# A four-layer graph network on one core: six of its 32 units keep their rows in SBUF between layers, and the output is laid out by node, then batch

## The chip, the core and the metric

The kernel runs on one core of one Trainium2 chip. A core has five engines that run their own instruction lists in order: TensorE (PE, matrix products, with its weight loads shown as PEld), VectorE (DVE), ScalarE (ACT), GpSimd (POOL) and SyncE (SP), which here only starts transfers. Transfers run on the core's 16 DMA engines, whichever list started them. SBUF is the on-chip memory of 128 partitions, PSUM the smaller one that PE writes to, DRAM the memory outside. The metric is the device time of one execution in microseconds (us); lower is better.

## The reference, cut to what matters

The input is x of shape (8, 2048, 128): 8 batches, 2048 nodes, 128 features. adj is a symmetric 0/1 matrix of 2048 x 2048 with ones on the diagonal and some 17 neighbours a node. Four layers follow each other: two of attention with a feed-forward part (layers 0 and 2, "MHA" here) and two of graph attention (layers 1 and 3, "GAT").

```python
# MHA, layers 0 and 2 (8 heads of 16)
Q, K, V = (h @ Wq), (h @ Wk), (h @ Wv)              # split into heads
scores = einsum('bnhd,bmhd->bhnm', Q, K) / sqrt(16)
attn = softmax(where(adj == 0, -inf, scores))
x = layer_norm(h + (attn @ V) @ Wo + bo, ln1_g, ln1_b)
x = layer_norm(x + relu(x @ W1 + b1) @ W2 + b2, ln2_g, ln2_b)

# GAT, layers 1 and 3
h = x @ W
e = leaky_relu((h @ a_src)[:, :, None] + (h @ a_dst)[:, None, :], 0.2)
att = softmax(where(adj == 0, -inf, e))
x = layer_norm(att @ h + x, ln_gamma, ln_beta)
```

## The kernel before, in words

The kernel (class Sparse; a class Dense stands behind a branch for matrices with too many neighbours, and is not run here) uses that adj is sparse. The nodes are cut into 32 units of 64 nodes (UNIT). Each unit has a list of its neighbours, built at the start from adj (block_list, unit_list), padded to 9 tiles of 128 slots (TILES), which are worked off in five steps of two, two, two, two and one tile.

Each layer first needs a table in DRAM with a row for each node: for MHA the keys and values of all 8 batches (8192 bytes), for GAT the projected features with two extra columns (4160 bytes). For each tile, POOL starts an indirect transfer (gather, line 1473) that fetches the 128 rows of the tile's slots from the table into a buffer kv of SBUF. There are six such buffers; one holds two tiles of an MHA layer or four of a GAT layer.

In MHA (attention) a step is: PE spreads the queries to the slots (qe, line 1546), DVE multiplies them with the keys (line 1558) and adds up over each head (line 1565), ACT takes the exponential (line 1575), POOL or DVE multiplies it with the values (line 1584), and PE adds the slots up for each node (line 1614). In GAT (graph) DVE makes the score e (line 1778, then 1785), ACT takes its exponential (1790), DVE folds it into the one-hot matrix of targets, giving w (line 1800), and PE adds up with w as its weights (line 1815). After its last step a unit is finished (after_attention, after_graph): products, normalisation, and at the end of layers 0 to 2 the unit's new rows x, transposed (xnew, from scaled, lines 1453 and 1455), and their projection for the next layer's table (project), which SP stores (line 1396). A layer's gathers need the whole table, so layers don't overlap, but for the loads of x and of the one-hot matrices.

The unit's rows x are needed again in the next layer, as queries' input and for the residual sum. So keep (line 1229) stores xnew, 256 KB, into a DRAM array xd, and in the next layer fetch (line 1241) loads it into one of four buffers x. Both transfers are on SP's list. In the last layer the normalised rows are stored into the output array of shape (8, 2048, 128) by two transfers of 128 KB a unit (line 1876), one for each half of the batches; a partition holds one node of one half, 4 batches x 128 features, and its four pieces of 512 bytes go to four places.

The order of all instructions is made beforehand by a planner (class Plan): each operation has a cost in us for each engine that may run it, a key (its due place), and the buffers it takes; the planner runs through them in simulated time and writes each engine's list in the order that results. A pool of buffers that is empty delays the operations that need one. The transfers have a cost in the plan too, so a transfer that is left out can move other operations. Within the lists the hardware runs in order, and semaphores do the waiting.

Names that the change touches: SBUF_BUFS (buffers of each pool; "w" has 3, "x1" 2 and "at" 1, the last two used in after_attention alone, 2 KB a partition each), keep, fetch, scaled, the fold in graph, the store in after_graph, falling (a constant row of 2048 numbers of 16 bits, read by block_list alone), zeros (a constant that nothing reads), and kernel, which makes the output array and hands it back.

Of the kernel before, what the change touches and what calls it, by code (L numbers as in the profile page):

```python
# [9 lines left out]
F32 = mybir.dt.float32  # L10
F32R = mybir.dt.float32r
BF16 = mybir.dt.bfloat16
# [8 lines left out]
P = 128  # L21
# [4 lines left out]
CH = 512  # L26
# [6 lines left out]
GROUP = 32  # L33
UNIT = 2 * GROUP
TG = 5
TILES = 2 * TG - 1
GS = TG * P
FIRST = 4
DEG = 40
KV = 4 * 1024 + 128  # L40
HOT = GS + 2 * TG * GROUP
WIDE = DEG + 5
STRIDE = 1000
LEAD = 60

SBUF_BUFS = {
    "kv": 6, "hot": 3, "hot8": 2, "x": 4, "q_sb": 2, "rows": 3, "at": 1, "r": 2, "x1": 2, "hidden": 1, "normed": 2,
    "xnew": 2, "trows": 2, "s": 2, "var": 2, "rstd": 2, "rc": 2, "te": 2, "e": 4, "w": 3,
    "cand": 2, "aux": 3, "unit_aux": 2, "some": 2, "rank_e": 2, "pick": 1,
}  # L50
BY_KEY = ("kv", "hot", "x", "q_sb", "acc")
# [14 lines left out]
class Dense:  # L66
# [460 lines left out]
    def batch(self, b):  # L527
        x = self.two.tile([P, self.NB, P], F32, name="x")
        self.nc.sync.dma_start(out=x, in_=self.x_in[b].rearrange("(t p) d -> p t d", p=P))
        for n, kind in enumerate(LAYERS):  # L530
            if kind is MHA:
                units = 2 * self.NB * (self.N // QC)
                gen = self.attention(x, n)
            else:
                units = self.NB * self.NC
                gen = self.graph(x, n)
            for u in gen:
                yield u / units
        self.nc.sync.dma_start(out=self.out[b].rearrange("(t p) d -> p t d", p=P), in_=x)

    def run(self):

# [199 lines left out]
class Sparse:  # L742
# [15 lines left out]
    def __init__(self, ctx, tc, x, xt, adj, w, out):  # L758
        self.tc, self.nc, self.w, self.xt_in, self.out = tc, tc.nc, w, xt, out
        self.B, self.N, _ = x.shape  # L760
        self.NB = self.N // P
        self.NU = self.N // UNIT
        self.HB = self.B // 2

        def pool(name, **kw):
            return ctx.enter_context(tc.tile_pool(name=name, **kw))

        self.nc.scalar.preload_act_table_set("natural_log_exp_and_others")
        self.const = pool("const", bufs=1)
# [24 lines left out]
        self.table = [Cell() for _ in LAYERS]  # L794

        self.xd = self.dram.tile([self.NU, P, CH], F32, name="xd")
        self.x_at = [Cell() for _ in range(self.NU)]
        self.hots = self.dram.tile([self.NU, P, HOT], F8, name="hots")
        self.hots_at = [Cell() for _ in range(self.NU)]
        self.ends_at = [None] * self.NU  # L800
        self.t = self.const.tile([P, self.NU, P // GROUP * self.HB], F32, name="t")
        self.t_at = [Cell() for _ in range(self.NU)]
        self.idx = self.const.tile([P, self.NU, TILES], I32, name="idx")
        self.idx_at = [Cell() for _ in range(self.NU)]

# [12 lines left out]
        self.rows_n = self.fixed("rows_n", float(self.N))  # L818
        self.huge = self.fixed("huge", 1e30)
        self.zeros = self.const.tile([GROUP, CH], BF16, name="zeros")  # L820
        self.nc.vector.memset(self.zeros, 0.0)

    def constants(self):
# [27 lines left out]
        for pattern, base, step, part in (  # L853
# [4 lines left out]
                part, pattern=pattern, base=base, channel_multiplier=step, allow_small_or_imprecise_dtypes=True  # L858
            )
        self.target = ramp("target", [P, GROUP], [[1, GROUP]], base=1)  # L860
        self.falling = const.tile([P, self.N], F16, name="falling")
        nc.gpsimd.iota(
            self.falling,
# [142 lines left out]
    def block_list(self, adj, i):  # L1006
# [21 lines left out]
                accum_out=self.seen[:, 0, i : i + 1],  # L1028
            ),
            key,  # L1030
            writes=[buf],
            port=True,
        )
# [190 lines left out]
            )  # L1224

    def keep(self, u, x, key):
        self.op(
            {"SP": 0.45},
            lambda e: e.dma_start(out=self.xd[u], in_=x.tile),
            key,  # L1230
            reads=[x],
            writes=[self.x_at[u]],
            dma=P * CH * 4,
        )

    def fetch(self, n, u, key):

        x = self.cell("x", [P, CH])
        self.op(
            {"SP": 0.45},  # L1240
            lambda e: e.dma_start(out=x.tile, in_=self.xd[u] if n else self.xt_in[u]),
            key,
            reads=[self.x_at[u] if n else self.gates[20]],
            writes=[x],
            dma=P * CH * 4,
        )
        hot = self.cell("hot", [P, HOT])
        if LAYERS[n] is MHA:
            hot8 = self.cell("hot8", [P, HOT], F8)
# [194 lines left out]
        else:  # L1444
            e.tensor_scalar(out, in_, by, None, ALU.mult)  # L1445

    def scaled(self, rows, gamma, beta, tag, key):
        x = self.cell(tag, [P, CH])
        ps = self.transposed(rows, key, x)

        def run(e):
# [9 lines left out]
            reads=[ps],  # L1461
# [163 lines left out]
    def after_attention(self, n, u, acc, sums, x, base):  # L1625
# [67 lines left out]
            )  # L1693
        add_to(r, ps, L["b2"], x1, key - 2)
        normed = self.norm(self.centred(r, key), key)
        x = self.scaled(normed, L["ln2_g"], L["ln2_b"], "xnew", key)
        self.keep(u, x, key)
        self.project(n + 1, u, x, key)

# [2 lines left out]
    def graph(self, n):  # L1702
# [3 lines left out]
        for u in range(self.NU):  # L1706
# [50 lines left out]
            for i, t in enumerate(steps):  # L1757
# [33 lines left out]
                    key - 4,  # L1791
                    writes=[e8],
                )
                w = cell("w", [P, 2, 2 * hb, GROUP])

                def fold(e, t=t, hot=hot, e8=e8, w=w, tiles=tiles):
                    oh = hot.tile[:, GS:HOT].rearrange("p (j t c) -> p j t c", j=2, t=TG)[:, :, t, :]
# [29 lines left out]
    def after_graph(self, n, u, outs, banks, acc, x, base):  # L1827
# [31 lines left out]
        )  # L1859
        normed = self.norm(r, key)  # L1860
        if n < len(LAYERS) - 1:
            x = self.scaled(normed, L["ln_gamma"], L["ln_beta"], "xnew", key)
            self.keep(u, x, key)
            self.project(n + 1, u, x, key)
        else:
# [8 lines left out]
            def store(e):  # L1874
                for part, nodes, hf in self.parts(u):
                    e.dma_start(
                        out=self.out[hf * hb : (hf + 1) * hb, nodes, :].rearrange("b p d -> p b d"),
                        in_=normed.tile[part],
                    )

# [102 lines left out]
```

## Time and profile before

| what | value |
|---|---|
| median of 3 runs (lowest, highest) | 3297.97 us (3291.01, 3309.48) |
| the profiled execution, its own time | 3274.86 us |
| its span, first to last instruction | 3273.1 us |
| PE, DVE, ACT, POOL busy, share of the span | 77%, 71%, 43%, 65% |
| moved by DMA | 1023.13 MB in 261243 packets |
| gathers (POOL's queue) | 864.44 MB, 70.8% of the 16 engines' time |
| SP's transfers | 154.56 MB, 13.8% |
| TensorE clock granted, mean | 0.875 of full speed |

The span has four stages. The lists and layer 0 go to about 1200 us, layer 1 to 1765, layer 2 to 2720, layer 3 to the end. Gathers of 8192-byte rows are those of layers 0 and 2, of 4160-byte rows those of 1 and 3. A line of "windows" gives for each engine the busy us in that stretch, then the granted clock, the mean busy share of the 16 DMA engines and the GB/s they moved. A line of "waits" reads: engine, line of the instruction that waited, what ended the wait, and then the total us, the number of waits and the longest one. In a line about a group of instructions, "x163" is how many there were, followed by shortest, median and longest duration in ns and the first and last start in us.

### The profile page before, as it was taken

The page shows a single profiled execution, that of the slowest core. Times are in us where ns is not written, and L with a number is a line of the kernel's source. Part 1 is how long each engine was busy: PE and PEld are TensorE (multiplying, and loading weights), DVE is VectorE, ACT ScalarE, POOL GpSimd, SP SyncE. Part 2 cuts the span into 40 slices and gives each one's busy share as a digit, 9 for nine tenths or more (in the row PEclk, how much of TensorE's full clock was granted, in tenths as well). Part 3 has the DMA queues.
Part 4 walks back from the last instruction along what each step waited for, and adds up shares of the span by engine and source line. Part 5 has one row for each costly group of instructions (what it writes and reads, how often), then busy time and mean ns, then how long its engine had stood idle before and what let it go on. Part 6 is the DMA issues. An engine that isn't in the chain of part 4 may idle for free. (4 is left out here: it accounts for less than half of the span.)

```text
span 3273.1 us, 63112 instructions
## 1 busy us (share of the span) xinstructions
PE 2517.2 (77%) x23560; PEld 1460.5 (45%) x23560; DVE 2308.8 (71%) x3740; ACT 1394.7 (43%) x4756; POOL 2131.7 (65%) x1454
## 2 busy tenths in 40 slices
PE   7768888888877767887876778888788785767675
PEld 5634444444333335565654333333333343555554
DVE  4779999898878753444445988988888883555555
ACT  4435554455444423444443344444444441333333
POOL 0268877787878725555553878877886854555662
PEclk8669999899999977889898899999999996778887
DMA  7858889788989849999997889989898866999994
GB/s 266 296 207 333 341 321 346 290 349 320 364 309 346 308 140 328 328 317 356 340 327 253 335 345 360 382 343 354 343 366 309 348 238 242 318 317 325 315 313 164
DMA packets 261243, 1023.13 MB, mean 313 GB/s; under 512 B 40192, under 2 KB 69632, under 8 KB 189024
## 3 DMA queue, kind: packets, MB, share of 16 engines
q0 software_dynamic: 166464, 864.44, 70.8%
q1 hardware_dynamic: 94464, 154.56, 13.8%
q8 instruction: 189, 3.10, 0.4%
q14 instruction: 126, 1.03, 0.1%
HBM read 978.59 MB, written 88.08 MB: 326 GB/s over the span
## 5 line engine op out<-in xcount | busy, mean ns | idle before, releaser
L1473 POOL DMA_INDIRECT kv<-table,idx x1152 | 1191.4, 1034 | 877.0 <-issue 359.9
L1584 POOL TENSOR_TENSOR kv<-kv 128x2048 f32<-128x2048 f32 (+1 forms) x259 | 927.2, 3593 | 85.3 <-ACT kv L1575 81.2
L1558 DVE TENSOR_TENSOR kv<-qe,kv 128x2048 f32<-128x2048 f32 (+1 forms) x320 | 662.6, 2071 | 156.5 <-DMA kv<-table,idx 104.6
L1565 DVE TENSOR_REDUCE s<-kv 128x128 f32<-128x2048 f32 (+1 forms) x320 | 659.9, 2062 | 8.5 <-ACT ps_e L1575 0.5
L1546 PE MATMUL qe<-q_sb,hot 32*128 32x512 f32 (+1 forms) x2304 | 401.8, 703 | 193.6 <-DVE kv L1558 183.1
L1614 PE MATMUL acc<-kv,hot 128*32 128x512 f32 x2560 | 362.2, 644 | 43.0 <-POOL kv L1584 32.2
L1815 PE MATMUL acc_q<-kv,w 128*32 128x129 f32 x5120 | 274.9, 315 | 103.7 <-issue 63.3
L1800 DVE TENSOR_TENSOR w<-hot,e 128x512 f32<-128x512 f32 (+1 forms) x384 | 221.8, 598 | 165.1 <-ACT e L1790 64.2
L1815 PEld LDWEIGHTS acc_q<-kv,w 128*32 128x32 f32 x5120 | 178.9, 124 | 183.5 <-issue 122.5
L1815 PE MATMUL acc<-kv,w 128*32 128x129 f32 x2560 | 154.8, 329 | 125.1 <-issue 88.3
L1546 PEld LDWEIGHTS qe<-q_sb,hot 32*128 32x128 f32 (+1 forms) x2304 | 106.8, 197 | 317.3 <-DVE kv L1558 243.6
L1575 ACT ACTIVATE kv<-s 128x128 f32<-128x128 f32 (+1 forms) x320 | 95.1, 297 | 311.2 <-DVE s L1565 173.7
L1410 ACT ACTIVATE junk<-ps_c 128x128 f32<-128x128 f32 x496 | 137.4, 277 | 189.9 <-PE ps_c L1311 140.0
L1289 ACT COPY trows<-ps_p 128x258 f32<-128x258 f32 (+1 forms) x231 | 108.7, 474 | 241.6 <-PE ps_p L1346 101.8
L1815 PE MATMUL sums<-kv,w 128*32 128x129 f32 x2560 | 169.9, 322 | 40.8 <-issue 39.9
L1614 PEld LDWEIGHTS sums<-kv,hot 128*32 128x32 f32 x2560 | 87.3, 115 | 211.5 <-issue 207.9
L1311 PE MATMUL ps_c<-centre,r 128*128 128x128 f32 x1024 | 151.6, 294 | 28.2 <-DVE r L1652 16.8
L1321 PE MATMUL ps_f<-x,W 128*128 128x512 f32 x256 | 155.5, 692 | 21.1 <-ACT x L1453 10.5
L1815 PEld LDWEIGHTS acc<-kv,w 128*32 128x32 f32 x2560 | 87.5, 127 | 172.8 <-issue 117.0
L1311 PEld LDWEIGHTS ps_c<-centre,r 128*128 128x128 f32 x1024 | 130.9, 200 | 68.3 <-DVE r L1652 34.2
L1443 ACT ACTIVATE normed<-ps_c,rstd 128x128 f32<-128x128 f32 x495 | 144.7, 369 | 8.4 <-DVE normed L1445 6.3
L1682 PE MATMUL ps_y<-hidden,W 128*128 128x512 f32 x256 | 143.3, 647 | 3.6 <-ACT hidden L1672 1.9
(169 smaller groups left out, 3903.4 us busy)
## 6 DMA issues: line engine op xcount, KB each, us to landing
table<-trows SPq DMA_DIRECT2D x128, 256.0 KB
xd<-xnew SPq DMA_DIRECT2D x96, 256.0 KB
x<-xd SPq DMA_DIRECT2D x96, 256.0 KB
kv<-table,idx POOLq DMA_INDIRECT x1152
table<-trows SPq DMA_DIRECT2D x128, 130.0 KB
kv<-adj_dram SPq DMA_DIRECT2D x16, 1024.0 KB
kv<-xt_dram SPq DMA_DIRECT2D x8, 1024.0 KB
x<-xt_dram SPq DMA_DIRECT2D x32, 256.0 KB
```

The source lines that it names most:

```text
L1311: e.matmul(ps.tile[:, cols], lhsT=flat(x.tile)[:, cols], rhs=self.centre, start=True, stop=True)
L1321: lambda e: e.matmul(ps.tile, lhsT=w, rhs=x.tile, start=True, stop=True),
L1443: e.activation(out, in_, AF.Copy, scale=by)
L1473: e.indirect_dma_start(out=rows(kv.tile, j), out_offset=None, in_=self.tables[n], in_offset=bass.IndirectOffsetOnAxis(ap=self.idx[:, u, co ...
L1546: e.matmul(qe.tile[:, j, hf, :], lhsT=hot.tile[rows, t * P : (t + 1) * P], rhs=q.tile[rows, :], start=True, stop=True,)
L1558: e.tensor_tensor(k, qe.tile[:, 0:tiles].rearrange("p j h c -> p (j h) c"), k, ALU.mult)
L1565: e.tensor_reduce(s.tile[:, 0 : tiles * heads].rearrange("p (q c) -> p q c", q=2 * tiles), k, axis=mybir.AxisListType.X, op=ALU.add,)
L1584: e.tensor_tensor(v, v, w.unsqueeze(3).to_broadcast([P, 2 * tiles, heads // 2, HD]), ALU.mult)
L1614: e.matmul(out[rows, :], lhsT=hot.tile[:, col : col + GROUP], rhs=rhs[:, 2 * (j % tiles) + hf, :], start=(t == 0), stop=(t == TG - 1),)
L1682: lambda e, f=f, ps=ps: e.matmul(ps.tile, lhsT=L["W2"][:, f, :], rhs=hidden.tile[:, f, :], start=(f == 0), stop=(f == FFN // P - 1),),
L1800: e.tensor_tensor(w.tile[:, j : j + tiles], oh[:, j : j + tiles].unsqueeze(2).to_broadcast(shape), e8.tile[:, 0:tiles].unsqueeze(3).to_bro ...
L1815: e.matmul(acc(b)[rows, :], lhsT=w.tile[:, j, hf * hb + b, :], rhs=both_rows(kv)[:, j % tiles, hf * hb + b, 1 : P + 2], start=first and b ...
```

## The change

Six units (4, 9, 14, 19, 24, 29; every KEPT-th, from the fifth on) each get a tile in SBUF that lasts for the whole kernel. Their rows are written there by scaled at the end of layers 0, 1 and 2, not into xnew; keep does nothing for them, and in layers 1 to 3 fetch hands out the tile and starts no load. Layer 0 still loads all its rows from the input. The room: the tiles of units 29 and 24 lie over falling (falling_at makes their first write wait for falling's readers), four tiles are new, the pool "w" is gone and zeros too. The fold's w takes a buffer of the pools "x1", "x1", "at" in turn. The output array becomes (2048, 8, 128), so that the four batches that a partition holds lie side by side, 2048 bytes; the host turns it back after the run.

```diff
+KEPT = 5
...
-    "xnew": 2, "trows": 2, "s": 2, "var": 2, "rstd": 2, "rc": 2, "te": 2, "e": 4, "w": 3,
+    "xnew": 2, "trows": 2, "s": 2, "var": 2, "rstd": 2, "rc": 2, "te": 2, "e": 4,
...
+        self.kept = {u: Cell() for u in range(KEPT - 1, self.NU, KEPT)}
+        for k, (u, c) in enumerate(list(self.kept.items())[::-1]):
+            if k < 2:
+                c.tile = self.falling.bitcast(F32)[:, k * CH : (k + 1) * CH]
+                self.falling_at.append(c)
+            else:
+                c.tile = self.const.tile([P, CH], F32, name=f"kept_{u}")
...
-        self.zeros = self.const.tile([GROUP, CH], BF16, name="zeros")
-        self.nc.vector.memset(self.zeros, 0.0)
...
     def keep(self, u, x, key):
+        if u in self.kept:
+            return
...
-        x = self.cell("x", [P, CH])
-        self.op(
-            {"SP": 0.45},
-            lambda e: e.dma_start(out=x.tile, in_=self.xd[u] if n else self.xt_in[u]),
...
+        if n and u in self.kept:
+            x = self.kept[u]
+        else:
+            x = self.cell("x", [P, CH])
+            self.op(
+                {"SP": 0.45},
+                lambda e: e.dma_start(out=x.tile, in_=self.xd[u] if n else self.xt_in[u]),
...
-    def scaled(self, rows, gamma, beta, tag, key):
-        x = self.cell(tag, [P, CH])
+    def scaled(self, rows, gamma, beta, tag, key, u=None):
+        x = self.kept[u] if u in self.kept else self.cell(tag, [P, CH])
...
-                w = cell("w", [P, 2, 2 * hb, GROUP])
+                w = cell(("x1", "x1", "at")[(u * TG + i) % 3], [P, 2, 2 * hb, GROUP], name="w")
...
-                        out=self.out[hf * hb : (hf + 1) * hb, nodes, :].rearrange("b p d -> p b d"),
+                        out=self.out[nodes, hf * hb : (hf + 1) * hb, :],
...
-    out = nc.dram_tensor("out_dram", x.shape, F32, kind="ExternalOutput").ap()
+    out = nc.dram_tensor("out_dram", [n_nodes, b, P], F32, kind="ExternalOutput").ap()
```

More of the change, by code (lines that the diff above doesn't have):

```diff
@@ L538, in batch @@
                 yield u / units
-        self.nc.sync.dma_start(out=self.out[b].rearrange("(t p) d -> p t d", p=P), in_=x)
+        self.nc.sync.dma_start(out=self.out[:, b, :].rearrange("(t p) d -> p t d", p=P), in_=x)
     def run(self):
@@ L860, in constants @@
         self.target = ramp("target", [P, GROUP], [[1, GROUP]], base=1)
+        self.falling_at = []
         self.falling = const.tile([P, self.N], F16, name="falling")
@@ L1030, in block_list @@
             key,
+            reads=self.falling_at,
             writes=[buf],
@@ L1236, in fetch @@
     def fetch(self, n, u, key):
-        x = self.cell("x", [P, CH])
-        self.op(
-            {"SP": 0.45},
-            lambda e: e.dma_start(out=x.tile, in_=self.xd[u] if n else self.xt_in[u]),
[L1242 to L1246, printed above, removed]
+        if n and u in self.kept:
[5 more added lines that the diff above has]
+                lambda e: e.dma_start(out=x.tile, in_=self.xd[u] if n else self.xt_in[u]),
+                key,
+                reads=[self.x_at[u] if n else self.gates[20]],
+                writes=[x],
+                dma=P * CH * 4,
+            )
         hot = self.cell("hot", [P, HOT])
@@ L1695, in after_attention @@
         normed = self.norm(self.centred(r, key), key)
-        x = self.scaled(normed, L["ln2_g"], L["ln2_b"], "xnew", key)
+        x = self.scaled(normed, L["ln2_g"], L["ln2_b"], "xnew", key, u)
         self.keep(u, x, key)
@@ L1861, in after_graph @@
         if n < len(LAYERS) - 1:
-            x = self.scaled(normed, L["ln_gamma"], L["ln_beta"], "xnew", key)
+            x = self.scaled(normed, L["ln_gamma"], L["ln_beta"], "xnew", key, u)
             self.keep(u, x, key)
@@ L1966 @@
     x = np.roll(np.asarray(inputs["x"]), -FIRST, axis=1)
-    b, n, _ = x.shape
-    xt = x.reshape(2, b // 2, n // UNIT, UNIT, P).transpose(2, 4, 1, 0, 3).reshape(n // UNIT, P, b * UNIT)
+    b, n_nodes, _ = x.shape
+    xt = x.reshape(2, b // 2, n_nodes // UNIT, UNIT, P).transpose(2, 4, 1, 0, 3).reshape(n_nodes // UNIT, P, b * UNIT)
     args = [give("x_dram", x), give("xt_dram", xt), give("adj_dram", np.roll(np.asarray(inputs["adj"]), (-FIRST, -FIRST), axis=(0, 1)))]
@@ L1981 @@
     r = run_bass_kernel_spmd(nc, [arrays], core_ids=[0])
-    return np.roll(r.results[0]["out_dram"], FIRST, axis=1)
+    return np.roll(r.results[0]["out_dram"].transpose(1, 0, 2), FIRST, axis=1)
```

## The prediction

> **What bounds the kernel now.** I read the page first, its slices and its queues, then the waits stage by stage, then counts of instructions in a stretch. The DMA engines look like the bound everywhere: in the page's second part the share is 8 or 9 tenths in most slices, and the queues sum to 85%.
>
> ```profile
> DMA  7858889788989849999997889989898866999994
> GB/s 266 296 207 333 341 321 346 290 349 320 364 309 346 308 140 328 328 317 356 340 327 253 335 345 360 382 343 354 343 366 309 348 238 242 318 317 325 315 313 164
> q0 software_dynamic: 166464, 864.44, 70.8%
> q1 hardware_dynamic: 94464, 154.56, 13.8%
> ```
>
> A high share is not yet a bound: somebody must wait for the data. So I asked for DVE's waits in a steady stretch of layer 1 (1300 to 1700 us) and in one of layer 2 (1850 to 2650 us). DVE is the first reader of gathered rows in both, by line 1778 in GAT and line 1558 in MHA.
>
> ```profile
> DVE e L1778 <- DMA kv<-table,idx: 0.3, 1, 0.3
> DVE kv L1558 <- DMA kv<-table,idx: 43.9, 26, 4.1
> ```
>
> In 400 us of layer 1 the score waited 0.3 us for a gather; in the stretch of layer 3 (2800 to 3200 us) such a wait is not among the twenty longest, which go down to 0.8 us. In layer 2 the wait is the longest that DVE has, 43.9 of 800 us. Counts say the same of GAT: from the layer's start to 1500 us POOL had issued 163 gathers and DVE had made 80 scores.
>
> ```profile
> L1473 POOL DMA_INDIRECT kv<-table,idx x163: 987/993/1512, 1206.3 to 1499.8; - x163
> L1778 DVE TENSOR_TENSOR e<-te,kv x80: 159/180/210, 1213.2 to 1497.3; 128x16 f32<-128x16 f32 x64, 128x8 f32<-128x8 f32 x16
> ```
>
> A unit has five scores and nine gathers, so 80 scores are 16 units or 144 gathers: POOL is 19 ahead, in buffers that hold 24. At 1600 us it is 219 against 111 scores (22 units and one step, some 199). The buffers are full; POOL waits until PE has used one up (in 1300 to 1700 us, 72.9 us for acc_q and 40.4 us for sums, both line 1815). From the trace's records of landings against starts of the scores, I work out that a gather had landed a median of 24 us or more before its score in all of layer 1 but its first step, and 23 us or more in layer 3. In MHA the same sum gives medians of 0.4 to 5.9 us, with 38 of 160 steps of layer 0 and 54 of 160 of layer 2 read within 0.6 us of landing.
>
> So GAT is paced by its chain through PE, DVE and ACT, and the transfers run under it. MHA is paced by DVE (92.39 and 97.20 us busy in 300 to 400 and 400 to 500 us, 86.75 in 2200 to 2300 us), with late gathers as its largest gap.
>
> **The change, part by part.** *Loads and stores of six units.* Removed are 6 stores at the end of each of layers 0, 1 and 2, and 6 loads in each of layers 1, 2 and 3: 36 transfers of 256 KB (0.262 MB), 9.4 of 1023.13 MB. Their price is taken from SP's queue in 1300 to 1700 us, which held only such loads and stores and the table's stores:
>
> ```profile
> q1 hardware_dynamic: 10432, 24.12, 16.9%
> ```
>
> 16.9% of 400 us is 67.6 us of all 16 engines for 24.12 MB, or 2.80 us a MB and 0.73 us for one transfer. The 36 are 26.4 us of DMA time: 4.4 in layer 0, 8.8 in layer 1, 8.8 in layer 2, 4.4 in layer 3. SP's list loses 36 starts of 0.33 us, and with them the waits for a free buffer x; what stands behind them there, table stores and other loads, can only start earlier.
>
> What reaches the end: in the GAT layers nothing, since gathers lie 19 tiles deep under the chain. That cover is missing in the first 60 us of each, until the buffers are full; at most one kept unit's load falls there, 0.73 us, and I put it at 0. Bounds 0 and 13.2 us for both layers. In layer 2 a transfer left out lets the gathers behind it land 0.73 us earlier, and this counts where DVE stands waiting. 54 of 160 steps do, a third: 8.8 x 0.34 = 3.0 us. Layer 0: 38 of 160, 4.4 x 0.24 = 1.1 us. Bounds 0 and 13.2 us.
>
> *The output stores.* 64 stores of 256 packets of 512 bytes become 64 of 64 packets of 2048 bytes; SP starts as many as before. With the queue empty otherwise, two of them near the end (3245 to 3252 us) show
>
> ```profile
> q1 hardware_dynamic: 544, 0.26, 16.9%
> ```
>
> that is 0.169 x 7 us = 1.18 us of all engines for 0.26 MB, 4.5 us a MB against 2.80. In the steady stretch 2800 to 3200 us SP's queue took 10.4% of 400 us, 41.6 us, for 13.13 MB; 25 loads of x at 0.73 us are 18.3 us of it, so 51 output stores (6.68 MB) took 23.3 us, 3.5 us a MB. Over 64 stores (8.39 MB) the saving is (3.5 - 2.8) x 8.39 = 5.9 us of DMA time at the one price, 14.3 at the other. It lies in layer 3 under the chain, where nobody waits for it, so again 0 of it, with 5.9 us as the bound that I take for the range, since the busy price holds while the queue is busy. Only the last two stores stand bare behind the last instruction: 0.26 MB x (4.5 - 2.8) = 0.4 us.
>
> The Trainium skill speaks against even this: "DMA: Bandwidth & Descriptors", Specifications, gives 512 B as the smallest transfer at line rate, so packets of 512 bytes would already be as good as larger ones. The trace disagrees with its 4.5 and 3.5 against 2.8 us a MB. By the rule the output's part would be 0 in every case, by the row 0.4 us.
>
> The same section puts the HBM limit of a core at about 358 GB/s. Layer 1 moves 334 to 341 GB/s, so by that rule it would run at 93 to 95% of the limit and every byte left out would count. The windows show 414 GB/s in 1780 to 1800 us and 369 in 1220 to 1240 us, so the row says that there is room. By the rule the sum below would be some 19 us larger.
>
> *The fold's buffers.* w had any of three buffers, now it has three in a fixed turn. The folds' turn is the order of their keys, so the third buffer back is the one freed first in both. DVE's waits at line 1800 for PE to give something back are 2.3 us (acc) and 1.0 us (sums) in 400 us of layer 1. Nothing else uses "x1" and "at" in a GAT layer, and a GAT layer's first gather needs the last MHA unit to be finished with them. Price 0; bounds 0 and, if those waits doubled, 3.3 us in 400 us, 8.5 us in the two layers' 1030 us.
>
> *The order.* Compared engine by engine, the lists are the same until late in layer 0 (PE's first moved instruction is about the 2910th of 11,800 matmuls). Behind that single steps of neighbouring units change places; POOL's list differs in some 40 places of 2,700 rows. No engine's work is added: PE has the same matmuls, ACT writes the kept tile where it wrote xnew, DVE loses one memset. A step put badly costs up to the longest waits of the GAT chain (te for ps_te in layer 1: 12 waits, 37.2 us, longest 6.0), one put well saves as much; I take 0, and bounds of -10 and +10 us, two or three such places.
>
> *Sum.* 3.0 + 1.1 + 0.4 = 4.5, say 5 us less. The span goes from 3273.1 to 3268 us and the profiled execution from 3274.9 to 3270. The median of the runs shown lies 23.1 us above the profiled execution, and I keep that distance: 3298 - 5 = 3293.
>
> **The rivals.** *The transfers are the pace after all.* For it: shares of 0.94 and 0.91 in 1400 to 1500 and 2900 to 3000 us, and that PE gets through 168 matmuls in 3230 to 3240 us, with a DMA share of 0.12, where it did 125 in 3210 to 3220 us at 0.97.
>
> ```profile
> 3210.00:3220.00 10.00, 7.61 (x125) 5.19 (x128) 5.32 (x22) 2.50 (x8) 6.05 (x6) 1.00 0.97 327
> 3230.00:3240.00 10.00, 8.45 (x168) 7.49 (x168) 6.37 (x19) 4.84 (x23) 0.00 (x0) 0.71 0.12 28
> ```
>
> Transfers could slow the chain in a way that no wait shows. Against it: the full buffers. Then 26.4 + 5.9 = 32 us would count, 3298 - 32 = 3266; I also put there any case in which most of it does, over 16.5 us.
>
> *The fixed turn of w stalls the chain.* Place: line 1800 in layers 1 and 3. If the fold waits for its named buffer until PE has finished a step that it earlier ran beside (0.65 us, 16 matmuls of line 1815), once a unit, 64 units lose 42 us: 3298 - 5 + 42 = 3335. It decides from half a wait a unit on: 64 x 0.33 = 21 us. For it: PE is the slowest link there, 82.22 us busy in 1400 to 1500 us. Against it: the present waits of 3.3 us in 400 us.
>
> *It doesn't do what it says:* excluded, SP's list has 36 fewer transfers and the stores are of one piece a partition.
>
> **How the numbers follow.** About 0.5%, 16.5 us, is what a measurement of this kernel can tell from no change; the three runs spread over 18 us. The forecast gets 0.53, the transfers as the pace 0.34, w and an unlucky order 0.13. These are also the chances of within, faster and slower. The predicted time is 3293. The range: down to 3264, which takes in the full saving of 32 us and 2 more for the order; up to 3312, which is 3298 with the fold's 8.5 and half of the order's 10. Its own range for the forecast alone is 3278 to 3308.
>
> **What would show it.** Right: SP's queue with 9.4 MB less and some 12,288 packets fewer for the output; layers 1 and 3 as long as before within 5 us, with a lower DMA share and POOL still 19 to 21 gathers ahead; DVE's wait at line 1558 a few us shorter in layer 2. Wrong: layer 3 shorter by 8 us or more with the same list of instructions (then the transfers did pace it), or waits at line 1800 on PE of tens of us (then w did).

## The result, and the profile after

The changed kernel takes 3318.78 us (median of 10 runs, 3314.26 to 3331.85) where the kernel before takes 3299.01 us in the same session (10 runs, 3283.97 to 3310.17). Run against run the ratio is 1.0043, with an interval of 1.0023 to 1.0063: slower by 0.43%, some 14 us; the two medians lie 20 us apart. The profiled executions lie further apart, 3314.4 us of span against 3273.1. One profile of each is too little for a change of this size, and below stages are compared over several profiles of the same lists.

What the change does to the transfers is as the prediction counted it. The lines are the page's count of all packets of the kernel after, and of SP's queue alone (packets, MB, share of the 16 engines):

```profile
DMA packets 243771, 1013.68 MB, mean 306 GB/s; under 512 B 39617, under 2 KB 52673, under 8 KB 171553
...
q1 hardware_dynamic: 76992, 145.12, 12.7%
```

SP's queue has 9.44 MB and 17,472 packets less: 12,288 for the output, the rest for the 36 transfers. The next two lines are the windows of layer 3 (2850 to 3050 us), before and then after, with PE, PEld, DVE, ACT and POOL busy, granted clock, DMA share, GB/s:

```profile
2850.00:3050.00 200.00, 141.76 (x2239) 105.34 (x2239) 105.77 (x349) 75.08 (x306) 118.97 (x113) 0.82 0.92 321
```
```profile
2850.00:3050.00 200.00, 140.06 (x2103) 104.52 (x2095) 100.75 (x332) 70.90 (x288) 111.69 (x107) 0.76 0.87 298
```

The DMA share falls from 0.92 to 0.87, and the layer gets no faster: 2103 matmuls pass in these 200 us, not more than the 2239 before. (The granted clock is lower too, 0.76 against 0.82, and in layer 3 this trace is the slowest of the three of these lists, so the table further down weighs more than this pair of lines.) DVE's waits in the kernel after say that nobody misses the gathers there either. From the start of layer 1 to 1500 us, gathers of POOL and scores of DVE:

```profile
L1486 POOL DMA_INDIRECT kv<-table,idx x164: 985/993/1469, 1199.1 to 1499.2; - x164
...
L1791 DVE TENSOR_TENSOR e<-te,kv x80: 165/179/257, 1206.1 to 1492.7; 128x16 f32<-128x16 f32 x64, 128x8 f32<-128x8 f32 x16
```

164 gathers are started and 80 scores have used 144: POOL is 20 ahead, where it was 19. DVE's fold (line 1813 now) has no wait on PE among its waits of 1.0 us or more in 1300 to 1700 us, where the kernel before had 2.3 and 1.0 us: the fixed turn of w stalls nothing.

In layer 2 something new appears. DVE's waits in 1850 to 2650 us, lines of the kernel before and then of the kernel after:

```profile
DVE kv L1558 <- DMA kv<-table,idx: 43.9, 26, 4.1
...
DVE t L1384 <- PE ps_p L1346: 9.6, 5, 5.9
...
DVE rc L1633 <- PE ps_q L1507: 7.4, 1, 7.4
...
DVE kv L1584 <- ACT ps_e L1575: 4.2, 9, 0.5
```
```profile
DVE kv L1571 <- DMA kv<-table,idx: 51.1, 37, 4.1
DVE kv L1597 <- ACT ps_e L1588: 19.2, 11, 9.1
...
DVE r L1665 <- PE ps_o L1334: 7.3, 2, 5.1
DVE rc L1646 <- PE sums L1627: 6.5, 1, 6.5
```

Both kernels have a place where a unit's finishing step rc stands too early in DVE's list and DVE waits for PE (7.4 us before, put down to ps_q; 6.5 us after, put down to the sums, at another unit). Before, a wait of 5.9 us at t follows 7 us later. The kernel after doesn't have that one, but it has a second place, with waits of 5.1 and 9.1 us. It lies near the end of the layer, and the timelines of DVE, ACT and PE show it:

```profile
2632.95 0.75 DVE L1665 SCALAR_TENSOR_TENSOR r<-ps_o,bo,x 128x512 f32<-128x512 f32 x1 [5.11 <-PE ps_o L1334]
...
2638.61 1.22 DVE L1578 TENSOR_REDUCE s<-kv 128x64 f32<-128x1024 f32 x1
2648.96 1.22 DVE L1597 TENSOR_TENSOR kv<-kv,ps_e 128x1024 f32<-128x1024 f32 x1 [9.14 <-ACT ps_e L1588]
2651.25 2.29 DVE L1571 TENSOR_TENSOR kv<-qe,kv 128x2048 f32<-128x2048 f32 x1 [1.06 <-PE qe L1559]
```
```profile
2641.05 0.25 ACT L1588 ACTIVATE kv<-s 128x64 f32<-128x64 f32 x1
...
2641.63 2.16 ACT L1456 ACTIVATE normed<-ps_c,rstd 128x128 f32<-128x128 f32 x8
2647.40 0.59 ACT L1524 COPY q_sb<-ps_q 128x512 f32<-128x512 f32 x1 [3.62 <-remote]
2647.89 0.79 ACT L1466 ACTIVATE xnew<-ps_t,ln_b,ln_g 128x512 f32<-128x512 f32 x1
2648.70 0.23 ACT L1588 ACTIVATE ps_e<-s 128x64 f32<-128x64 f32 x1
```
```profile
2643.07 1.16 PE L1520 MATMUL ps_q<-Wq,x 128*128 128x128 f32 x8 [1.54 <-ACT normed L1456]
...
2649.09 2.09 PE L1559 MATMUL qe<-q_sb,hot 32*128 32x512 f32 x8
```

DVE's sums over heads (line 1578) were ready at 2639.8. The exponential that DVE's next instruction needs (ps_e) takes 0.23 us, but in ACT's list it stands behind two normalisations at once and a copy of the next unit's queries (q_sb), before which ACT stood 3.62 us. Lists run in order, so ACT reaches it at 2648.70, and DVE stands for 9.1 us. The next unit's multiply, behind it in DVE's list, could hardly have run earlier: it waits another 1.06 us for PE's qe, which needs that same copy. So the next unit's queries come as late as the exponential. PE makes their product (ps_q) only at 2643.07, behind a wait for the normalisations. No transfer shows in this chain, and its order is the planner's; but what ended ACT's 3.62 us the profile doesn't name (PE's records of the product end 3 us earlier), so for that part no cause is shown.

### The profile page after: what moved, and what is told of

Same layout as the page of the kernel before. It is cut to its first block, busy times and chain, and to the rows that moved or that the text cites. A ratio compares the mean times of both kernels' runs of the same rounds, so it can differ in the third digit from the quotient of the medians.

```text
span 3314.4 us, 63000 instructions
## 1 busy us (share of the span) xinstructions
PE 2528.6 (76%) x23560; PEld 1468.8 (44%) x23560; DVE 2303.2 (69%) x3737; ACT 1388.9 (42%) x4757; POOL 2129.7 (64%) x1455
## 3 DMA queue, kind: packets, MB, share of 16 engines
q14 instruction: 126, 1.02, 0.1%
## 5 line engine op out<-in xcount | busy, mean ns | idle before, releaser
L1743 DVE TENSOR_TENSOR te<-ps_te,empty 128x32 f32<-128x32 f32 x128 | 18.4, 186 | 194.7 <-remote 103.6
```

## The experiments

The names in the expectations: A or A1, the new order of the lists is what costs, and any order is a draw; A2, orders planned without the left-out transfers are worse as such; B, the fold's turn of w; C, the output's layout; D, the kept tiles or transfers; P, the pace of the GAT layers differs by chip. Each session ran its kernels and the kernel before on one chip. RATE is a constant in the planner (what it thinks the DMA engines move). It adds and removes no work; it changes the plan, that is the order, and for a few operations also which of two engines runs them: in rate27's trace 5 of the 128 copies trows<-ps_p of 128x512 moved from DVE to ACT, in the change's trace the 2 copies at<-ps_t that DVE had, and of other kinds one to three each. "Order" below means the plan with these.

| run | lists in the order of | data path | before, us | ratio (interval) |
|---|---|---|---|---|
| the change | its own | after | 3299.0 | 1.0043 (1.0023, 1.0063) |
| after_again | the change | after | 3281.1 | 1.0023 (1.0002, 1.0044) |
| after_third | the change | after | 3285.7 | 1.0036 (1.0014, 1.0058) |
| old_order | before | after | 3278.1 | 1.0010 (0.9988, 1.0032) |
| old_order_2 | before | after | 3285.7 | 1.0005 (0.9982, 1.0028) |
| w_only | before | fold's turn | 3278.1 | 0.9988 (0.9968, 1.0008) |
| out_only | before | output's layout | 3278.1 | 1.0008 (0.9989, 1.0027) |
| kept4 | its own | 4 units kept | 3278.1 | 0.9986 (0.9964, 1.0007) |
| stores_planned | its own | after | 3281.1 | 1.0034 (1.0014, 1.0054) |
| rate25 | RATE 25 | before | 3281.1 | 0.9996 (0.9976, 1.0016) |
| rate27 | RATE 27 | before | 3281.1 | 0.9945 (0.9922, 0.9968) |
| old27_2 | that of rate27 | after | 3285.7 | 0.9931 (0.9907, 0.9956) |
| extra_loads_2 | before | before, 96 more loads | 3285.7 | 1.0032 (1.0008, 1.0056) |
| extra_loads | before | before, 96 more loads | 3050.9 | 1.0147 (1.0114, 1.0180) |
| traffic_back | the change | after, 36 transfers back | 3050.9 | 1.0012 (0.9991, 1.0033) |
| old27 | that of rate27 | after | 3050.9 | 0.9926 (0.9898, 0.9954) |
| after27 | after, RATE 27 | after | 3050.9 | 0.9919 (0.9889, 0.9950) |
| after27_2 | after, RATE 27 | after | 3043.6 | 0.9939 (0.9915, 0.9962) |
| after25 | after, RATE 25 | after | 3043.6 | 0.9942 (0.9921, 0.9964) |

The last six ran on chips where the kernel before itself takes 3044 to 3051 us. They are read apart.

**The data path in the old order.** old_order keeps the tiles, the fold's turn and the output's layout, but the planner still counts the left-out transfers and their buffers, so that the lists of PE, DVE, ACT and POOL are those of the kernel before (in the traces DVE, ACT and POOL run the same operations in the same sequence, but for the memset of zeros).

```diff
-        if u in self.kept:
-            return
-            lambda e: e.dma_start(out=self.xd[u], in_=x.tile),
+            lambda e: None if u in self.kept else e.dma_start(out=self.xd[u], in_=x.tile),
...
+        x = Cell("x", lambda: self.kept[u].tile) if held else self.cell("x", [P, CH])
+            lambda e: None if held else e.dma_start(out=x.tile, in_=self.xd[u] if n else self.xt_in[u]),
...
-        x = self.kept[u] if u in self.kept else self.cell(tag, [P, CH])
+        x = Cell(tag, lambda: self.kept[u].tile) if u in self.kept else self.cell(tag, [P, CH])
```

> All of the change's data path (six kept units, no transfers for them, w in the buffers of x1 and at, the new output layout), but the planner still counts the left-out transfers and their buffers, so every engine's list stands in the order of before. Theory A (the new order of the lists costs the time): ratio to before 0.995 to 1.000, that is the forecast's 5 us gain and no more; layers 1 and 3 as long as before. Theory B (w's fixed turn) and theory D (kept tiles where they lie in SBUF): 1.004 as the whole change. Theory C (output layout): 1.004, all of it in layer 3.

> The change's data path in the order of the kernel before, once more. Theory P: on a chip of some 3280 us 0.999 to 1.002; on a chip of 3051 us the gain of the transfers left out stands alone: 0.991 to 0.996. Rival (transfers are worth nothing on either): 1.000.

1.0010 and 1.0005: neither the 0.4% nor a gain. In after_third's session the two kernels, which differ in nothing but the order, stand at 1.0005 and 1.0036; the intervals overlap, and the medians of 12 runs each, 3291.0 and 3296.1 us, lie 5 us apart. For comparison the kernel after was run twice more:

> The changed kernel once more, for its ratio on the chip and in the minutes of the three beside it. Theory A (the planner's new order costs the time): 1.003 to 1.007, against 1.001 [0.9988, 1.0032] of old_order, which is the same data path in the old order. Rival: it was the chip, and here it is within 0.002 of 1.

> The kernel after once more. Theory A1 with P: on a chip of some 3280 us 1.002 to 1.005, as in the two comparisons so far; on a chip of 3051 us the transfers left out are worth something in the GAT layers as well: 35 us less work for the DMA engines at the 0.65 of it that extra_loads cost there, some -20 us, against some +14 us for the order: 0.996 to 1.001, below traffic_back's 1.0012. Rival (the change costs the same everywhere): 1.002 to 1.005 on both.

It was slower each time, 1.0023 and 1.0036, by less than at first.

**One part alone.** w_only and out_only are the kernel before with one edit each, and their order is that of before. kept4 keeps four units (14, 19, 24, 29; w has its own pool, the output its old layout) and has an order of its own.

```diff
-                w = cell("w", [P, 2, 2 * hb, GROUP])
+                w = cell(("x1", "x1", "at")[(u * TG + i) % 3], [P, 2, 2 * hb, GROUP], name="w")
```
```diff
-                        out=self.out[hf * hb : (hf + 1) * hb, nodes, :].rearrange("b p d -> p b d"),
+                        out=self.out[nodes, hf * hb : (hf + 1) * hb, :],
```
```diff
-        self.kept = {u: Cell() for u in range(KEPT - 1, self.NU, KEPT)}
+        self.kept = {u: Cell() for u in list(range(KEPT - 1, self.NU, KEPT))[-4:]}
```

> Before, with w alone moved into the buffers of x1 and at; the lists' order is that of before. Theory B (a fold waits for its named buffer): 1.004 or more, about 14 to 20 us, in layers 1 and 3, with DVE's waits at the fold on PE grown. Theories A, C and D: 1.000, within 5 us.

> Before, with the output layout alone changed; the lists' order is that of before. Theory C (the 2048-byte packets at a pitch of 4096 bytes are slower, or collide with gathers): 1.003 to 1.006, all in layer 3. Theories A, B and D: 0.998 to 1.000: 0.4 us from the last two stores, up to 6 us if layer 3's transfers pace it.

> Before, with four units kept (14, 19, 24, 29; more don't fit beside a pool of its own for w), w in its own three buffers and the output as before. The planner gives a third order, nearer to that of before (PE's list differs in 656 compared lines, where the whole change differs in 2238). Theory A: any ratio from 0.995 to 1.005, since it is another order; no growth where the order is that of before. Theory D (kept tiles): 1.003, two thirds of the whole change's loss. Theories B and C: 0.997 to 1.000.

0.9988, 1.0008 and 0.9986: none of the parts costs anything that can be told from nothing (B, C and D fall).

**The order alone.** The kernel before with another RATE has the same instructions and transfers, in another order (the expectations count 2628 and 3970 lines of difference in PE's list, against 2238 for the change).

```diff
-    RATE = 16 * 26e3
+    RATE = 16 * 27e3
```

> Before, unchanged but for one number in the planner, the speed at which it believes the DMA engines move bytes (25 in place of 26): the same instructions and transfers in another order (PE's list differs in 2628 compared lines, about as much as the whole change's 2238). Theory A1 (any reshuffle moves the time by some tenths of a per cent, up or down): within 0.994 to 1.006, either side. Theory A2 (a plan that counts fewer or cheaper transfers is the worse one): with dearer transfers 0.994 to 1.000. If neither order nor plan matters: 1.000, within 0.001.

> Before, with 27 in place of 26 as the planner's speed of the DMA engines: the plan counts every transfer 4% cheaper, the hardware moves the same (PE's list differs in 3970 compared lines). Theory A1: within 0.994 to 1.006, either side, no relation to rate25. Theory A2: 1.003 to 1.008, slower as the whole change is, and opposite to rate25. If order doesn't matter: 1.000, within 0.001.

rate27 is faster by 0.55%, rate25 is as fast as before. So an order alone is worth more than all that the change does to the data. A2's 1.003 to 1.008 for rate27 is out. Of the three settings only 27 gains, so no direction shows; that the gain comes from where the stalls happen to fall, and not from a truer figure, is argued and not shown. stores_planned is the change with a planner that counts the left-out stores but not the loads, and so with a fourth order:

```diff
-        if u in self.kept:
-            return
...
-            lambda e: e.dma_start(out=self.xd[u], in_=x.tile),
+            lambda e: None if u in self.kept else e.dma_start(out=self.xd[u], in_=x.tile),
```

> The change's data path; the planner counts the six units' left-out stores as before but no longer their loads and their buffers x. PE's list differs from that of before in 594 compared lines and from the changed kernel's in 2032. Theory A: near old_order, 0.998 to 1.003, not the whole change's 1.004. Theory D (kept tiles themselves, or the data path as a whole): 1.004.

It came out at 1.0034, above what A expected and near the 1.004 that D foretold; D falls all the same, since old_order has this data path too. Why this order is slow is seen only in part (its layer 2, 955.7 us, has the stall of the kernel before, and its layer 1 took 574.8 us). That the better order carries the changed data path was asked of old27, which is old_order with RATE 27 and runs the very lists of rate27:

> The change's data path in the order of rate27, once more. On the chip of 3051 us it measured 0.9926; rate27, the same order with the old data path, 0.9945 on a chip of 3281 us. Theory A1 with P: on a chip of some 3280 us 0.993 to 0.997, as rate27 there; on a chip of 3051 us again 0.990 to 0.995. Rival (on chips of 3280 us the changed data path costs 0.4%): 0.998 to 1.000 there.

0.9931: 22 us faster than the kernel before, 33 us faster than the change in the same session, with all of the change's data path. Of all pairs this one shows most plainly that the lists, and not the data path, make the difference. DVE's waits in layer 2 of that run hold neither stall at its former size:

```profile
DVE kv L1567 <- DMA kv<-table,idx: 44.9, 32, 4.0
...
DVE kv L1593 <- ACT ps_e L1584: 5.8, 5, 3.8
```

**Where an order wins and loses.** Stages, from the first gather of a layer to the first of the next (layer 3 to the last product with w), worked out from the starts of the 1152 gathers in the traces taken on chips of 3278 to 3299 us; mean, and lowest to highest:

| lists of | traces | layer 0 | layer 1 | layer 2 | layer 3 |
|---|---|---|---|---|---|
| before | 5 | 1070.6 (1060.9, 1078.0) | 569.2 (566.7, 574.4) | 950.0 (948.1, 955.3) | 536.4 (529.2, 540.6) |
| the change | 3 | 1061.9 (1060.6, 1063.0) | 570.3 (565.1, 580.4) | 961.2 (960.2, 963.1) | 542.2 (537.6, 549.8) |
| rate27 | 2 | 1075.5 (1072.2, 1078.8) | 559.5 (559.1, 559.8) | 944.5 (940.1, 948.8) | 526.8 (526.6, 527.0) |

(before: the kernel before, w_only, out_only, old_order, old_order_2; the change: its first trace, after_again, after_third; rate27: itself and old27_2.) Layer 2 is the one stage whose times for the two orders don't overlap: the change loses 11.2 us there in the mean. DVE's waits at ps_e, ps_o and rc stand in every trace of this order as well (rc early in the layer, the other two at its end), as the lines of after_third show:

```profile
DVE kv L1597 <- ACT ps_e L1588: 14.2, 11, 7.5
...
DVE rc L1646 <- PE sums L1627: 9.2, 1, 9.2
...
DVE r L1665 <- PE ps_o L1334: 7.1, 2, 4.9
```

At ps_e the order of before has 4.2 us, with 0.5 us as the longest, in each of its five traces. Summed over the layer, DVE stood 139 to 146 us in these five and 153 to 156 us in the three of the change. Its waits for gathers are alike (56 to 67 us in both sets), and ps_e alone is 10 to 15 us longer; the other waits nearly cancel. In layer 0 the change's order is 9 us faster in the mean, in layer 3 some 6 slower, both within the spread of single traces. The sums of the means differ by +9.4 us for the change and -19.9 us for rate27, close to what the ratios say (+8 to +14, and -18 to -23 us). But the +9.4 hangs on the change's first trace: the four stages of the other two sum to 3125 to 3126 us, as the mean of the five does, because layers 0 and 1 give back what layer 2 loses. So the traces show the loss in layer 2, and the runs the loss in all. That the stall at ps_e is worth its 9 us was not tried by moving it alone: ps_e holds one of two PSUM buffers that the units' finishing shares, and one instruction can't be moved without others.

**More traffic instead of less.** To test that the GAT layers don't wait for transfers, the reverse was done to the kernel before, in its own order: each load of x in layers 1 to 3 is followed by a second one into a constant that nobody reads any more. 25.2 MB and, at 0.73 us each, 70 us of the DMA engines: 2.7 times what the change takes away.

```diff
+    def bring(self, e, x, n, u):
+        e.dma_start(out=x.tile, in_=self.xd[u] if n else self.xt_in[u])
+        if n:
+            at = u % 2 * CH
+            e.dma_start(out=self.falling.bitcast(F32)[:, at : at + CH], in_=self.xd[u])
```

> The kernel of extra_loads once more (96 more loads of x in layers 1 to 3, 70 us of all 16 engines, order untouched). On the chip of its first run, where the kernel before takes 3051 us and DVE waits for gathers in layer 1 (72 us in 1300 to 1500), it cost 1.47%. Theory P (the pace of the GAT layers differs by chip: gathers there, the chain where the prediction's trace was taken): on a chip where the kernel before takes some 3280 us and layer 1 shows no DVE wait for gathers, 0 to 0.5%; on a chip of 3051 us again 1.2 to 1.8%. Rival T (transfers are the pace on every chip): 1.2 to 2.1% on either.

On a chip of 3286 us they cost 0.32%, 10.5 us, and in the one trace layer 2 alone is longer (959.6 us against a mean of 950.0); layers 1 and 3 took 569.1 and 532.4 us, not a microsecond longer than without them (569.2 and 536.4). The window of layer 1 in the kernel before, then the same window and its only wait for a gather in extra_loads_2:

```profile
1300.00:1500.00 200.00, 160.58 (x2244) 117.24 (x2240) 85.14 (x300) 89.70 (x322) 110.02 (x107) 0.88 0.94 332
```
```profile
1300.00:1500.00 200.00, 160.95 (x2284) 117.90 (x2284) 88.11 (x316) 91.89 (x325) 113.13 (x109) 0.90 0.98 356
...
DVE e L1784 <- DMA kv<-table,idx: 0.3, 1, 0.3
```

The DMA share rises from 0.94 to 0.98, PE gets through as many matmuls, and the layer has room for it. On the other kind of chip the same kernel had cost 1.47%, 45 us:

> The kernel before, its order untouched on PE, DVE, ACT and POOL; each of the 96 loads of x in layers 1 to 3 is followed by a second load of the same 256 KB into the constant falling, which nobody reads any more. It adds 25.2 MB and, at 0.73 us each, 70 us of all 16 engines: 2.7 times what the change leaves out. Theory A1 (only the order of the lists matters, transfers run under the chain in GAT and count for a third in layer 2, as the prediction had it): 32 x 0.73 x 0.34 = 8 us, ratio 1.000 to 1.004, layers 1 and 3 within 10 us of the kernel before. Rival (transfers are the pace): 70 us, ratio about 1.021, layers 1 and 3 longer by some 23 us each.

DVE waited 72.0 us for gathers in the same 200 us, and neither theory had that number. So the remaining kernels of that kind of chip were compared with each other:

```diff
+            self.op(
+                {"SP": 0.0},
+                lambda e: e.dma_start(out=x.tile, in_=self.xd[u]),
+                key,
+                reads=[self.x_at[u], self.last_x],
+            )
```

> The kernel after, its order untouched on PE, DVE, ACT and POOL, with the 36 stores and loads of the six kept units put back on SP's list at no cost in the plan (a kept tile is stored to xd, and loaded from there into itself in the next layer). Theory A1 (the order costs): as slow as the kernel after, ratio 1.002 to 1.007, layer 2 again 955 to 965 us. Rival D (leaving the transfers out, or the kept tiles, is what costs): with the transfers back the time returns to that of the kernel before, 0.998 to 1.001. Rival A0 (the transfers left out gain their 5 us, the order costs more): slower than the kernel after by 0.15%, 1.004 to 1.006.

> The whole data path of the change (kept tiles, fold's turn, output layout), with the planner still counting the transfers left out and its RATE at 16 x 27e3, so that PE, DVE, ACT and POOL run the very lists of rate27, which measured 0.9945 with the data path of before. Theory A1: 0.992 to 0.997, as rate27. Rival D (the changed data path costs time of its own): 0.998 to 1.002, some 0.4% above rate27. If the 4.5 us of the prediction show: 0.993.

> The kernel after with RATE at 16 x 27e3 and nothing else: a new order, planned as the change plans it (without the transfers left out). Theory A1 (each order is a draw, within some 0.5% of the kernel before either way): anything from 0.994 to 1.005, and where it is slow, a stall of 5 us or more at the end of a unit of layer 2 shows it. Rival A2 (a plan that doesn't count the left-out transfers is worse): 1.002 or more again.

> The kernel after with RATE at 16 x 27e3 and nothing else, once more (0.9919 on the chip of 3051 us, where it can't be told from the transfers' gain). Its lists are near those of rate27 (PE 807 lines of difference against 1494 to the kernel after). Theory A1: on a chip of some 3280 us 0.992 to 0.998, with none of the stalls of layer 2 of the kernel after (DVE for ps_e in 1850 to 2650 us under 8 us, longest under 4). Rival A2 (planning without the transfers left out is worse): 1.001 or more there.

> The kernel after with RATE at 16 x 25e3 and nothing else: a third order for the same work. Theory A1 (each order is a draw, RATE no knob with a direction): rate25 was 0.9996 on a chip of 3281 us, so 0.996 to 1.004 on such a chip, which side is not foretold; on a chip of 3051 us 0.7% lower. If it were the RATE that counts, in one direction, it would be slower than the kernel after: 1.005 or more.

traffic_back, the change's order with its 36 transfers put back (the edit above, and the stores likewise), took 475.3 + 415.3 = 890.6 us in layers 1 and 3; the four kernels without the transfers, old27, after27, after27_2 and after25, in three different orders, took 873.3 to 876.5 us. extra_loads, in the order of before with 64 loads more in these layers, took 929 us, 39 us more than traffic_back for 47 us of transfers. The 14 to 17 us are about the full price of the loads and stores left out there (13.2 us by the prediction's 0.73 us each), if the change's order counts there as little as those three do among themselves; the two weren't told apart. With the 72.0 us of waits this says that on that kind of chip the transfers are the pace of the GAT layers, and that the prediction's first rival is right there. The change itself didn't run there, so whether it is faster on such a chip than the kernel before is open; traffic_back's 1.0012 lies between the ranges of A1 and D and decides nothing between them. Its layer 2 took 950.4 us, below the 955 to 965 that A1 expected, but the longest of the six on those chips (the others 934.0 to 947.8), with the wait at ps_e again (13.3 us, longest 6.0). Against A2 speak old27 and after27, with the same data path and RATE in one session, planned with and without the left-out transfers: 0.9926 and 0.9919. On chips of 3280 us that pair wasn't run. after27's 0.9919 is below A1's range, in which the worth of the transfers on such a chip was not counted; after25 and after27_2 can't be split into order and transfers either.

## Why the prediction was wrong

**Transfers in layers 1 and 3: right.** They were put at 0 because POOL is 19 gathers ahead. The share of the DMA engines fell, POOL stayed 20 ahead, and neither fewer transfers nor 47 us more of them (64 x 0.73) shortened or lengthened these layers on chips like that of the prediction's trace (layer 1 without the transfers, in the old order: 574.4 and 570.2 us, against 566.7 to 567.3 with them). **The rival that they are the pace** is false there and true on the other kind of chip, which no view of the one trace could tell.

**Layers 2 and 0, -3.0 and -1.1 us: not refuted, too small to be seen.** The share of a third, taken from the steps that DVE reads as they land, gives 32 x 0.73 x 0.34 = 8 us for the 32 extra loads of layer 2, and 9.6 us were measured, in one trace of a stage that differs by up to 7 us between traces of one order. Layer 0 wasn't tried. The gain itself doesn't show: a gain of 4.5 us would be 0.9986, and old_order's 1.0010 and 1.0005 have intervals that begin at 0.9988, just above it, and at 0.9982. The sign that was named for it, DVE's wait for gathers in layer 2 a few us shorter, could not have served: 51.1, 44.4 and 40.9 us in three traces of the change, 43.9, 38.3 and 49.7 in three of the old order.

**Output and last stores, 0 and -0.4 us:** out_only's 1.0008 has nothing against the 0 but can't show 0.4 us, and the traces say that the 0.4 isn't there. Two of the last stores, alone in the queue, took in the kernel after (3288 to 3295 us)

```profile
q1 hardware_dynamic: 160, 0.26, 16.4%
```

with packets of 2048 bytes, where the prediction's line has 16.9% of as many us with packets of 512. So its 4.5 us a MB is what a store costs there that is alone in the queue, with either kind of packet, and of the prediction's two comparisons with 2.8 only that of the 3.5 sets a busy queue against a busy one. While the queue is busy the longer packets are the cheaper ones: worked out from the records of layer 3, 2.7 us a MB in the kernel after against 3.4 before.

**The fixed turn of w, 0:** right, w_only 0.9988 and no new wait at the fold; the rival of 3335 us is false.

**The step that failed is the order: "I take 0, and bounds of -10 and +10 us".** The lists of the change cost about 10 us against the same data path in the old lists (1.0036 against 1.0005 in one session; 5 us by the medians), at or near the edge of the bound, and it was the largest term of the sum, not one to be set to 0. The price of a place was taken from the longest waits of the GAT chain, 6.0 us; the place that was worst lies in layer 2, where DVE, the pace of that layer, stood 9.1 and 5.1 us behind two in-order lists, and the stall at rc that the old order had at another unit was exchanged for one of the same size rather than won back. Nor were the bounds wide enough: with no other change an order was worth -18 us (rate27). A sum of 5 us beside a term of plus or minus 18 can't carry a forecast of the sign. The order doesn't account for all of the 3318.78 us, though, where 3293 was forecast and 3312 was the end of the range: the first session has 14 us by the ratio and 20 by the medians, the two repeats some 8 and 12 by the ratio. The ten runs of the change in that session were granted a clock of 0.865 in the mean, those of the repeats 0.872 and 0.871; whether that is the rest stays open.

## What to carry to other kernels

Where a planner writes the lists, every edit that touches its costs, buffers or transfers draws a new order, and the draw can be larger than the edit: run the edit in the old order (count what was left out in the plan, but don't issue it) and the new order with the old data, before either is credited. A few orders of the same work are worth trying for their own sake; here one constant of the planner gave 0.55%, and 0.7% together with the changed data path, which beats both kernels. A DMA share over 0.9 decides nothing by itself: adding transfers to an unchanged order tells which stage waits for them, on the chip where it is run.

## What the runs showed of the hardware

The same kernel took 3263 us on one chip and 3024 on another, and most of the difference lies in the layers whose gathers are of 4160-byte rows. The windows and longest waits of layer 1, of the same lists, old27_2 and then old27:

```profile
1300.00:1500.00 200.00, 165.91 (x2281) 120.54 (x2271) 86.49 (x312) 88.62 (x317) 114.06 (x109) 0.87 0.94 337
...
PE acc_q L1824 <- issue: 15.4, 37, 1.1
PE sums L1824 <- issue: 6.4, 17, 1.0
PE acc L1824 <- issue: 5.3, 11, 1.3
```
```profile
1300.00:1500.00 200.00, 162.67 (x2786) 128.52 (x2774) 108.33 (x387) 111.44 (x396) 132.32 (x132) 0.91 1.02 402
...
DVE e L1787 <- DMA kv<-table,idx: 69.4, 54, 3.4
```

On the first chip PE stops between matmuls of line 1824 for nothing that the profile shows, 27 us in 200; on the second no such wait is listed, PE gets through 2786 matmuls instead of 2281 (22% more, at a granted clock of 0.91 against 0.87), and with 402 GB/s moved in all the gathers become what DVE waits for. Layers 1 and 3 took 559.8 and 527.0 us on the first, 466.4 and 410.1 on the second, layer 2 940.1 and 940.5. In the DMA records of this stretch a packet of 4160 bytes took 185 ns on the first and 167 on the second in the mean, with a median of 161 on both, so the first has more slow ones. An argument for the rival in the prediction, that PE slows as the DMA share rises, gets no support: on the second chip PE ran fastest at a share of 1.02, and on a chip of the first kind 2284 matmuls passed at 0.98 against 2244 at 0.94. What stops PE on the first chip is open; no run here bears on it. The Trainium skill, "DMA: Bandwidth & Descriptors", Specifications, puts the HBM limit of a core at about 358 GB/s; 402 GB/s over 200 us is above it. That limit is half of what two cores share, by the same row, and this kernel runs on one core.
